# Layer 0's preparation: two blocks' destination terms formed on VectorE, their values deferred

## The chip, the cores and the metric

The kernel runs on one core of one Trainium2 chip. The metric is device time in microseconds for one launch, the median over runs. A profiled execution of the same program gives the trace that this document reads. In its lines PE is TensorE (PEld its weight loads), DVE is VectorE, ACT is ScalarE, POOL is GpSimd and SP is SyncE.

## What is computed

The reference is a stack of four graph layers over 4096 nodes with 256 features and one sparse 0/1 adjacency matrix. Each layer normalises its input and applies ReLU first. Only layer 0 is touched:

```python
h = jnp.maximum(_layernorm(x, axis=-1), 0.0)
Wh = h @ W
e = Wh @ a_src + (Wh @ a_dst).T          # logit of (row i, column j)
e = jnp.where(e > 0, e, 0.2 * e)         # leaky ReLU
e = jnp.where(adj > 0, e, -9.0e15)
attn = jax.nn.softmax(e, axis=1)
h_attn = attn @ Wh
```

After this comes the dense rest of layer 0, then layers 1 (mean over neighbours), 2 (attention again) and 3 (dot-product attention).

## The kernel before

Nodes are handled in 32 tiles of 128, and four tiles make a block, so there are 8 blocks (`NB = 8`, `BT = 4`, `NT = 32`). Layer 0's attention has two stages.

**The preparation**, the subject of this case, is the function `block0(b)`, run for the 8 blocks as staggered generators. For a block it takes the statistics of its four rows of x on VectorE (`stats_of`, L130 and L131). It subtracts the mean with its sign turned, xs = mean − x: two of the four tiles on GpSimd (the first and the last), one on ScalarE (L803), one on VectorE (all the others at L807). It computes 1/std on GpSimd (`rstd_of`, L121 and L124, into `pl_rs`). TensorE transposes the block (L153, into `tp`), and ScalarE evacuates the transposes with ReLU and scale −1 (L155, into `hT`). TensorE then multiplies each tile with `w2` (L162, into `mm`), which holds W and two more columns W·a_src and W·a_dst, and ScalarE scales the product by 1/std into `v` (`project`, L310). So `v` holds, for each node, its value row and its terms src and dst. The two extra columns of `w2` are formed by VectorE in `columns` (L296), for which TensorE spreads the two vectors (L289).

Between these steps the adjacency is unpacked. `load` asks for units of 128 rows by 1024 columns through GpSimd's DMA queue (L639). `fresh` transposes a unit on TensorE (L649, into `cT`), and ScalarE turns it with an Exp into a code that separates edges from non-edges (L654, into `turned`). A group of 4 row tiles has 16 units.

VectorE then runs, for each group, over all 32 column tiles and keeps the running minimum of (code − dst): `reach` (L335 and L337, into `run`, and the last one into `run_sb`). This gives each row's maximum of dst over its neighbours. Column tile j needs its dst and the code of its quarter. Transposed and reduced (`top`: L358, L362 to L367), it becomes two numbers for each row, which are spread over the partitions by TensorE (L372, L387) and copied (L376, L392).

**The loop** `run` then forms for each pair of column tiles the logits on VectorE (L412), subtracts the code on GpSimd (L418, L420), takes Exp on ScalarE (L482) and accumulates the weighted values on TensorE (L505, into `acc`). While it does so for one group, `ahead` unpacks the units of the next group and VectorE reaches over it.

Each engine takes its instructions in one fixed order. That order is made when the program is built: a scheduler places the instructions that the Python code records, and `tc.issue_after(x)` asks that what is recorded inside it stands behind x on its queue. `psm` has two buffers for the products `mm`, so TensorE can be at most two tiles ahead of their evacuation. `work` has two buffers, `small` four.

Of the kernel before, what the change touches and what calls it, by code (L numbers as in the profile page):

```python
# [11 lines left out]
F32 = mybir.dt.float32  # L12
# [31 lines left out]
def kernel(ctx: ExitStack, tc: tile.TileContext, w: dict, out: bass.AP):  # L44
# [101 lines left out]

    def transposed_block(work, pst, h, tag, turned=None):

        hT = work.tile([P, KD, BW], F32, tag=tag, name=tag)
        for k in range(KD):  # L150
            ps = pst.tile([P, BW], F32, tag="tp", name="tp")
            for i in range(BT):
                nc.tensor.transpose(ps[:, ts(i, P)], h[:, i, ts(k, P)], ident)  # L153
            if turned is not None:
                turned.append(nc.scalar.activation(hT[:, k, :], ps, AF.Relu, scale=-1.0))  # L155
            else:
                evac(k, hT[:, k, :], ps)
        return hT

    def products(ps, lhsT_of, rhs_of, n):  # L160
        for k in range(n):
            nc.tensor.matmul(  # L162
                out=ps, lhsT=lhsT_of(k), rhs=rhs_of(k), start=(k == 0), stop=(k == n - 1)
            )

    PE, DVE = "PE", "DVE"
# [48 lines left out]
    class Attention:  # L215
        def __init__(self, es, tag, slope, lag, n_y, blocks, turned, finish, ps_top=None):
            self.tag, self.slope, self.lag, self.n_y = tag, slope, lag, n_y
            self.turned, self.finish = turned, finish

            self.links = []  # L220
            self.blocks = [{"at": at, "n": n} for at, n in blocks]
            vp = es.enter_context(tc.tile_pool(reuse_waits="tile", name=f"{tag}_sd", bufs=1))
            self.sdst = vp.tile([P, NT], F32, name="sdst")
            self.cdst = vp.tile([P, NT], F32, name="cdst")
            self.own_dst, self.held = None, False
# [65 lines left out]
        def columns(self, work):  # L291
            w2, a2 = self.w2, self.a2
            for k in range(KD):
                for v in range(2):
                    junk = work.tile([P, D], F32, tag="junk", name="junk")
                    nc.vector.tensor_tensor_reduce(  # L296
                        junk, w2[:, k, 0:D], a2[:, ts(v, D)], 1.0, 0.0, ALU.mult, ALU.add,
                        w2[:, k, D + v : D + v + 1],
                    )

        def project(self, b, hT, psm, rs=None):

            for i in range(BT):
                ps = psm.tile([P, D + 2], F32, tag="mm", name="mm")
                products(ps, lambda k: hT[:, k, ts(i, P)], lambda k: self.w2[:, k, :], KD)
                row = self.v[:, b * BT + i, 1 : D + 3]
                if rs is None:
                    nc.scalar.copy(row, ps)
                else:
                    nc.scalar.mul(row, ps, rs[:, i : i + 1])  # L310

        def slopes(self, at):
            dst = self.dst_of(at)
            nc.vector.tensor_scalar(self.sdst[:, at], dst, self.slope, None, ALU.mult)
            nc.vector.tensor_scalar(self.cdst[:, at], dst, 1.0 - self.slope, None, ALU.mult)

        def reach(self, n, tie=None):
# [9 lines left out]
            for j in range(c, c + 2):  # L327
                code = self.turned(b, j // QT)[:, :, j % QT, :]
                dst = self.dst_of(slice(j, j + 1)) if tie is None else tie[:, j - c : j - c + 1]
                to = st["run"]  # L330
# [19 lines left out]
        def top(self, b, pool=None, tag="top"):  # L350
# [6 lines left out]
            for r in range(n):  # L357
                nc.tensor.transpose(ps[:, r, :], st["run"][:, r, :], ident)  # L358
            yield DVE
# [18 lines left out]
            if b < self.spread:  # L378

                yield PE  # L380
                for v in range(2):
# [4 lines left out]
                    for k in range(n):  # L386
                        nc.tensor.matmul(  # L387
                            out=ps[:, k, :], lhsT=self.picks[0 : 2 * n, v * n + k, :], rhs=abT,
# [16 lines left out]
        def logits(self, y, b, c, mask):  # L405
# [5 lines left out]
            for k in range(2):  # L411
                nc.vector.scalar_tensor_tensor(  # L412
                    y[k], st["ab"][:, 0, :, :], self.cdst[:, c + k : c + k + 1],
                    st["b"], ALU.add, ALU.max,
                )
                if y.apart:
                    eng = (nc.vector, nc.gpsimd)[k]
                    ins = eng.tensor_tensor(y[k], y[k], mask[:, :, c % QT + k, :], ALU.subtract)  # L418
            if not y.apart:
                ins = nc.gpsimd.tensor_tensor(  # L420
                    y.both, y.both, mask[:, :, c % QT : c % QT + 2, :], ALU.subtract
                )
            return ins

# [5 lines left out]
        def run(self, es, goal, n_acc, ahead=lambda n: None):  # L430
# [15 lines left out]
            for n in range(len(pairs) + LAG):  # L446
                between = False
                if n < len(pairs):
# [21 lines left out]
                    ys[n] = y  # L470
                    masked = self.logits(y, b, c, self.turned(b, c // QT))
                    if n < PPB and not self.tied:
                        with tc.issue_after((self.newest if n > LAG else masked).ins):
                            ahead(n)
                        while self.reached <= m:
                            self.reach(self.reached)
                if n >= LAG:
                    b, c = pairs[n - LAG]
                    y = ys.pop(n - LAG)
                    with tc.issue_after(self.gate.ins) if self.gate and c else ExitStack():  # L480
                        for k in range(2):
                            self.newest = nc.scalar.activation(  # L482
                                y[k], y[k], AF.Exp,
                                bias=self.sdst[:, c + k : c + k + 1],
                            )
                    if c == 0:
                        accs[b] = [
# [88 lines left out]
    FIRST = UPB  # L576
    FRESH = 3
    UNITS0 = (0, 2, 4, 6, 8, 11, 14, 16)
    PAIRS0 = (0, 0, 0, 2, 4, 6, 8, 12, 16)
    PACE = (LAG0 + 1, 2 * PPB + 4)  # L580
    with ExitStack() as l0:
# [10 lines left out]
        with ExitStack() as es:  # L592
# [14 lines left out]
            def turned_of(k, q):  # L607
# [12 lines left out]
            att.picks, att.spread = picks.tile([n, n, P], F32, name="picks"), 2  # L620
            nc.vector.tensor_copy(
                att.picks,
                ident[0:n, 0:n].rearrange("k (v o) -> k v o", o=1).broadcast_to([n, n, P]),
            )
            adj_p = es.enter_context(tc.tile_pool(reuse_waits="tile", name="adj", bufs=8))
# [5 lines left out]
            ]  # L631
            raw, made = [], [0]

# [7 lines left out]
            def fresh(up_to):  # L641

                load(up_to)
                for g in range(made[0], up_to):
# [3 lines left out]
                    for i in range(QW // BW):  # L648
                        nc.tensor.transpose(ps[:, ts(i, P)], words[:, ts(i, P)], ident)  # L649
                    if (b, q) not in turned:  # L650
# [117 lines left out]
            with ExitStack() as ps_:  # L768
# [11 lines left out]
                for at, n in [(0, BT // 2), (BT // 2, BT // 2)] + [  # L780
# [5 lines left out]
                    )  # L786

                def block0(b):
                    xb = xs[:, ts(b, BT), :]
                    mv = small.tile([P, BT, 2], F32, tag="pl_mv", name="pl_mv")  # L790
                    for i in range(BT):
                        st = None
                        if b == 0:

                            st = work.tile([P, D], F32, tag="junk", name="junk")[:, 0:6]
                        stats_of(small, xb[:, i, :], mv[:, i, :], "pl", st)


                    for i in range(BT):
                        mean = mv[:, i, 0:1]  # L800
                        if i == 1 or b == 0 and i == BT - 1:
                            with tc.issue_after(evacs[-1].ins) if evacs else ExitStack():
# [3 lines left out]
                        else:  # L806
                            (nc.gpsimd if b and i in (0, BT - 1) else nc.vector).tensor_scalar(  # L807
                                xb[:, i, :], xb[:, i, :], mean, -1.0, ALU.subtract, ALU.mult
                            )
                    rs = rstd_of(small, mv, BT, "pl")  # L810
                    if b == 0:
                        att.spread_row(a_row, psm)
                        att.columns(work)
                    load(min(3 * b + 6, UPB + RB))
                    yield
                    hT = transposed_block(work, pst, xb, "hT", turned=evacs)
                    fresh(UNITS0[b])
                    yield
                    att.project(b, hT, psm, rs)
                    yield  # L820
# [5 lines left out]
                run_staggered([block0(b) for b in range(NB)], 2)  # L826
                for _ in att.top(0, pst, "tp"):
                    pass
                att.held = False
                att.slopes(slice(0, NT))  # L830
                fresh(UPB + 2)
# [726 lines left out]
```

## Time and profile before

| what | value |
|---|---|
| runs, us | 2859.99, 2856.09, 2857.85 |
| median, us | 2857.85 |
| the profiled execution's own time, us | 2859.48 |
| its span, us | 2857.7 |
| granted TensorE clock, mean over the span | 0.994 |
| busy: PE / DVE / ACT / POOL | 98% / 67% / 44% / 35% |
| chain that ended last: PE | 84% |

The span is what the trace covers; 1.78 us of the profiled time lie around it. The profiled execution is 1.63 us above the median. TensorE is busy nearly all the time but for the first slices, so the shares over the whole span say little of the preparation, which ends some 70 us after the start: there one has to read windows and the order of time.

### The profile page before, as it was taken

To read this page: it belongs to the slowest core of one execution; us is meant where nothing else is said; L and a number is where in the kernel's file an instruction comes from. 1 tells how busy PE (TensorE), PEld (TensorE's weight loads), DVE (VectorE), ACT (ScalarE), POOL (GpSimd) and SP (SyncE) were. 2 spreads that over 40 slices of the span, in tenths; PEclk is the share of its full clock that TensorE was granted. 3 is DMA by queue.
4 is the path that set the end of the run, shared out by engine and by line. 5 is a ranking of instruction groups with operands and counts; after the bars stand their busy time and mean duration, and the time that the engine had idled before them with its cause. 6 is when DMAs were issued, how large, how long until landed. Compare 5 with 4: busy or idle time off the path is not lost.

```text
span 2857.7 us, 33849 instructions
## 1 busy us (share of the span) xinstructions
PE 2802.7 (98%) x12614; PEld 2298.7 (80%) x12614; DVE 1910.2 (67%) x3441; ACT 1249.4 (44%) x1883; POOL 1005.0 (35%) x901
## 2 busy tenths in 40 slices
PE   7999999999999999999999999999999999999999
PEld 5888888856666666888788888878888888888888
DVE  6877777345555555677799999547666665666563
ACT  6666654366777753787444444441211121112111
POOL 5767766445555553221076666610000000000000
PEclk9999999999999999999999999999999999999999
DMA  7988884322233312799322221021110101111100
GB/s 170 148 176 167 164 165 138 86 19 26 26 28 30 29 15 79 149 203 202 143 82 91 94 82 52 8 71 47 47 38 33 63 33 38 34 53 43 37 4 8
DMA packets 102327, 223.05 MB, mean 78 GB/s; under 512 B 10562, under 2 KB 52276, under 8 KB 91156
## 3 DMA queue, kind: packets, MB, share of 16 engines
q1 hardware_dynamic: 63072, 181.39, 17.9%
q0 software_dynamic: 37536, 35.03, 15.5%
q10 hardware_dynamic: 1556, 4.49, 0.4%
q8 instruction: 99, 1.62, 0.2%
q14 instruction: 64, 0.52, 0.1%
HBM read 264.85 MB, written 56.68 MB: 113 GB/s over the span
## 4 chain that ended last, share of the span: by engine, by line
PE 84%; DVE 5%; POOL 3%; ACT 3%; issue 3%; DMA 1%; POOLq 0%; ACTq 0%; DVEq 0%; SPq 0%
PE acc L505 22%; PE mm L162 19%; PE acc L1490 16%; PE s L162 15%; PE acc L1225 8%; POOL y L420 2%; DVE run L337 2%; PE tp L877 2%; DVE y L412 1%; ACT y L482 1%; ACT turned L654 1%; PE q_ps L162 1%; DMA ab_row<-l_ab_d 1%; POOL adj_t L639 1%; DMA l_ab_d<-abT_sb 0%
## 5 line engine op out<-in xcount | busy, mean ns | idle before, releaser
L505 PE MATMUL acc<-v,y 128*128 128x257 f32 x4096 | 913.8, 382 | 8.4 <-ACT y L482 7.6
L505 PEld LDWEIGHTS acc<-v,y 128*128 128x128 f32 x4096 | 772.6, 191 | 116.0 <-ACT y L482 8.6
L420 POOL TENSOR_TENSOR y<-y,turned 128x1024 f32<-128x1024 f32 x255 | 543.0, 2136 | 288.7 <-DVE y L412 194.9
L482 ACT ACTIVATE y<-y,sdst 128x512 f32<-128x512 f32 x512 | 342.5, 714 | 377.7 <-POOL y L420 375.4
L1490 PE MATMUL acc<-v,y 128*128 128x257 f32 x2048 | 454.5, 380 | 0.4 <-DVE rden L1498 0.4
L162 PE MATMUL s<-qT,hT 128*128 128x256 f32 x2048 | 445.2, 379 | 0.7 <-ACT qT L1438 0.7
L1483 ACT ACTIVATE y<-y 128x1024 f32<-128x1024 f32 x128 | 132.5, 1055 | 714.8 <-DVE y L1482 710.5
L162 PEld LDWEIGHTS s<-qT,hT 128*128 128x128 f32 x2048 | 389.0, 190 | 54.1 <-ACT qT L1438 1.3
L1490 PEld LDWEIGHTS acc<-v,y 128*128 128x128 f32 x2048 | 387.1, 190 | 55.9 <-issue 0.8
L412 DVE SCALAR_TENSOR_TENSOR y<-ab_row,cdst,b 128x512 f32<-128x512 f32 x512 | 362.6, 742 | 70.1 <-PE acc L505 61.4
L192 ACT ACTIVATE sign<-a,limits 128x1024 bf16<-128x1024 fp8e5 x256 | 293.7, 1147 | 7.1 <-DMA a<-in_adj_dram 1.1
L1452 DVE SCALAR_TENSOR_TENSOR y<-code,s 128x512 f32<-128x512 bf16 x256 | 175.8, 687 | 101.1 <-PE s L162 101.0
L337 DVE SCALAR_TENSOR_TENSOR run<-turned,v,run 128x512 f32<-128x512 bf16 x240 | 180.2, 751 | 48.1 <-ACT turned L654 45.7
L1482 DVE TENSOR_TENSOR y<-y,top 128x1024 f32<-128x1024 f32 x128 | 146.2, 1214 | 30.4 <-PE top L1476 30.4
L183 POOL DMA_DIRECT2D a<-in_adj_dram x128 | 76.0, 597 | 248.1 <-ACT sign L192 210.4
L1459 DVE TENSOR_TENSOR mx<-mx,y 128x512 f32<-128x512 f32 x224 | 154.8, 691 | 7.5
L654 ACT ACTIVATE turned<-cT,log_wide 128x1024 bf16<-128x1024 fp8e5 x128 | 139.2, 1105 | 27.2 <-PE cT L649 26.9
L337 DVE SCALAR_TENSOR_TENSOR run<-turned,y,run 128x512 f32<-128x512 bf16 x193 | 145.2, 753 | 3.0
L162 PE MATMUL mm<-kept 128*128 128x512 f32 x288 | 130.4, 595 | 0.0
L1225 PE MATMUL acc<-early,eq 128*128 128x512 f32 x512 | 126.4, 397 | 0.3 <-DVE o L1234 0.3
L1498 DVE RECIPROCAL rden<-acc 128x1 f32<-128x1 f32 x32 | 5.2, 163 | 177.8 <-PE acc L1490 177.8
L1225 PE MATMUL acc<-late,eq 128*128 128x512 f32 x512 | 122.4, 391 | 0.0
(256 smaller groups left out, 3130.8 us busy)
## 6 DMA issues: line engine op xcount, KB each, us to landing
codesT<-turned SPq DMA_DIRECT2D x50, 1024.0 KB, 5.9
turned<-codesT SPq DMA_DIRECT2D x36, 1024.0 KB, 4.8
code<-codesT SPq DMA_DIRECT2D x128, 256.0 KB, 6.5
code<-codesT SPq DMA_DIRECT2D x64, 512.0 KB, 6.4
adj_t<-in_adj_dram POOLq DMA_DIRECT2D x128, 128.0 KB, 6.0
a<-in_adj_dram POOLq DMA_DIRECT2D x128, 128.0 KB, 4.6
xt<-in_x_dram SPq DMA_DIRECT2D x8, 512.0 KB, 3.2
ab_row<-l_ab_d ACTq DMA_DIRECT2D x8, 512.0 KB, 3.6
```

The lines of the kernel that those rows point to most:

```text
L162: nc.tensor.matmul(out=ps, lhsT=lhsT_of(k), rhs=rhs_of(k), start=(k == 0), stop=(k == n - 1))
L192: nc.scalar.activation(sign, self.came[g], AF.Sign, bias=limits[:, v : v + 1], accum_out=over[:, t, v, q : q + 1],)
L337: nc.vector.scalar_tensor_tensor(to, code, dst, st["run"], ALU.subtract, ALU.min)
L412: nc.vector.scalar_tensor_tensor(y[k], st["ab"][:, 0, :, :], self.cdst[:, c + k : c + k + 1], st["b"], ALU.add, ALU.max,)
L420: ins = nc.gpsimd.tensor_tensor(y.both, y.both, mask[:, :, c % QT : c % QT + 2, :], ALU.subtract)
L482: self.newest = nc.scalar.activation(y[k], y[k], AF.Exp, bias=self.sdst[:, c + k : c + k + 1],)
L505: nc.tensor.matmul(out=accs[b][r], lhsT=y1[j % 2][:, r, :], rhs=self.v[:, j, 0 : D + 1], start=(j == 0), stop=(j == NT - 1),)
L654: nc.scalar.activation(ct.rearrange("p (g k) i -> p g k i", k=4), ps.bitcast(F8).rearrange("p (g i k) -> p g k i", i=P, k=4), AF.Exp, scal ...
L1225: nc.tensor.matmul(out=acc, lhsT=eqs[c // (NT // 2)][:, ts(c % (NT // 2), P)], rhs=v1[c // BT][:, c % BT, :, :], start=(c == 0), stop=(c = ...
L1452: nc.vector.scalar_tensor_tensor(y[:, :, c : c + 2, :], st["code"][:, :, c : c + 2, :], -BIG / UNIT, ps, ALU.mult, ALU.add,)
L1459: nc.vector.tensor_tensor(mx, mx, y[:, :, c : c + 2, :], ALU.max)
L1490: nc.tensor.matmul(out=accs[r], lhsT=st["y"][:, r, c, :], rhs=v3[:, c, :], start=(c == 0), stop=(c == NT - 1),)
```

## The change

In layer 0's preparation:

- For the last two blocks (b = 6 and 7, `near`) the mean is subtracted with its own sign and ReLU is applied in the same instruction, no tile of them goes to ScalarE, and `transposed_block` is given scale +1.
- For these blocks dst is not read from the product with `w2`. VectorE multiplies each of the eight tiles with a row `wa` (W·a_dst laid along the free axis on all partitions) and sums (`tensor_tensor_reduce`, changed L853), then scales by 1/std (changed L856), into `near`. `reach` reads `near` for the last eight column tiles.
- `wa` comes from two more TensorE products in block 1 (changed L864) and a ScalarE copy (changed L868).
- The products and values of the two blocks are recorded after all the blocks, behind the newest unit transposed, and the last tile behind the transposes of `top`.
- In blocks 4 and 5 two of the four value tiles are scaled out of PSUM by VectorE instead of ScalarE (changed L314).
- `columns` comes ahead of the statistics of blocks 1 to 7 in VectorE's queue, and the copy to `picks` behind it. `load` asks for up to 24 units in the preparation instead of 20.
- In the loop, `ahead` of the first four pairs comes behind the Exp of the first pair, `reach` stands behind the newest logits, and the two subtractions of the first pair are recorded in the other order.

The diff, cut to what matters:

```diff
-    def transposed_block(work, pst, h, tag, turned=None):
+    def transposed_block(work, pst, h, tag, turned=None, sign=-1.0):
...
-                turned.append(nc.scalar.activation(hT[:, k, :], ps, AF.Relu, scale=-1.0))
+                turned.append(nc.scalar.activation(hT[:, k, :], ps, AF.Relu, scale=sign))
...
-        def project(self, b, hT, psm, rs=None):
-
-            for i in range(BT):
+        def project(self, b, hT, psm, rs=None, rows=range(BT), shared=False):
+
+            for i in rows:
...
+                elif shared and i % 2:
+                    nc.vector.tensor_scalar(row, ps, rs[:, i : i + 1], None, ALU.mult)
                 else:
                     nc.scalar.mul(row, ps, rs[:, i : i + 1])
...
-                dst = self.dst_of(slice(j, j + 1)) if tie is None else tie[:, j - c : j - c + 1]
+                if b == 0 and self.near is not None and j >= NT - NEAR * BT:
+                    at_near = j - NT + NEAR * BT
+                    dst = self.near[:, at_near : at_near + 1]
+                else:
+                    dst = self.dst_of(slice(j, j + 1)) if tie is None else tie[:, j - c : j - c + 1]
...
                     if n < PPB and not self.tied:
-                        with tc.issue_after((self.newest if n > LAG else masked).ins):
-                            ahead(n)
-                        while self.reached <= m:
-                            self.reach(self.reached)
+                        if n > LAG:
+                            with tc.issue_after(self.newest.ins):
+                                ahead(n)
+                        with tc.issue_after(self.on_dve.ins):
+                            while self.reached <= m:
+                                self.reach(self.reached)
...
+                    if n == LAG and not self.tied:
+                        with tc.issue_after(self.newest.ins):
+                            for k in range(n + 1):
+                                ahead(k)
...
+    NEAR = 2
...
+                att.near = wp.tile([P, NEAR * BT], F32, name="near")
+                wa = wp.tile([P, D], F32, name="wa0")
+                formed, kept_back = [], []
+
                 def block0(b):
                     xb = xs[:, ts(b, BT), :]
+                    near = b >= NB - NEAR
                     mv = small.tile([P, BT, 2], F32, tag="pl_mv", name="pl_mv")
-                    for i in range(BT):
+                    with tc.issue_after(formed[0].ins) if formed else ExitStack():
+                        for i in range(BT):
...
                     for i in range(BT):
                         mean = mv[:, i, 0:1]
-                        if i == 1 or b == 0 and i == BT - 1:
+                        eng = nc.gpsimd if b and i in (0, BT - 1) else nc.vector
+                        if near:
+                            eng.tensor_scalar(
+                                xb[:, i, :], xb[:, i, :], mean, 0.0, ALU.subtract, ALU.max
+                            )
+                        elif i == 1 or b == 0 and i == BT - 1:
...
                     if b == 0:
                         att.spread_row(a_row, psm)
-                        att.columns(work)
-                    load(min(3 * b + 6, UPB + RB))
+                        formed.append(att.columns(work))
+                        with tc.issue_after(formed[0].ins):
+                            nc.vector.tensor_copy(att.picks, one_of)
+                    load(min(3 * b + 6, UPB + 2 * RB))
...
-                    att.project(b, hT, psm, rs)
+                    if near:
+                        to = att.near[:, (b - NB + NEAR) * BT :][:, 0:BT]
+                        for i in range(BT):
+                            junk = work.tile([P, D], F32, tag="junk", name="junk")
+                            nc.vector.tensor_tensor_reduce(
+                                junk, xb[:, i, :], wa, 1.0, 0.0, ALU.mult, ALU.add, to[:, i : i + 1]
+                            )
+                        nc.vector.tensor_tensor(to, to, rs, ALU.mult)
+                        kept_back.append((b, hT, psm, rs))
+                    else:
+                        att.project(b, hT, psm, rs, shared=b >= NB - NEAR - 2)
+                    if b == 1:
+                        ps = psm.tile([P, D], F32, tag="mm", name="mm")
+                        for k in range(KD):
+                            col = att.w2[:, k, D + 1 : D + 2]
+                            nc.tensor.matmul(
+                                out=ps[:, ts(k, P)], lhsT=col.broadcast_to([P, P]), rhs=ident,
+                                start=True, stop=True,
+                            )
+                        nc.scalar.copy(wa, ps)
...
                 run_staggered([block0(b) for b in range(NB)], 2)
-                for _ in att.top(0, pst, "tp"):
+                att.slopes(slice(0, NT - NEAR * BT))
+                att.slopes(slice(NT - NEAR * BT, NT), att.near)
+                with tc.issue_after(newest_unit[0].ins):
+                    att.project(*kept_back[0])
+                    att.project(*kept_back[1], rows=range(0, BT - 1))
+                chain = att.top(0, pst, "tp")
+                for _ in range(2):
+                    next(chain)
+                with tc.issue_after(att.on_pe.ins):
+                    att.project(*kept_back[1], rows=range(BT - 1, BT))
+                for _ in chain:
                     pass
                 att.held = False
-                att.slopes(slice(0, NT))
                 fresh(UPB + 2)
```

More of the change, by code (lines that the diff above doesn't have):

```diff
@@ L161, in products @@
         for k in range(n):
-            nc.tensor.matmul(
+            last = nc.tensor.matmul(
                 out=ps, lhsT=lhsT_of(k), rhs=rhs_of(k), start=(k == 0), stop=(k == n - 1)
             )
+        return last
     PE, DVE = "PE", "DVE"
@@ L224, in __init__ @@
             self.cdst = vp.tile([P, NT], F32, name="cdst")
-            self.own_dst, self.held = None, False
+            self.own_dst, self.held, self.near = None, False, None
             self.tied = False
@@ L295, in columns @@
                     junk = work.tile([P, D], F32, tag="junk", name="junk")
-                    nc.vector.tensor_tensor_reduce(
+                    last = nc.vector.tensor_tensor_reduce(
                         junk, w2[:, k, 0:D], a2[:, ts(v, D)], 1.0, 0.0, ALU.mult, ALU.add,
@@ L299, in columns @@
                     )
-        def project(self, b, hT, psm, rs=None):
-            for i in range(BT):
+            return last
+        def project(self, b, hT, psm, rs=None, rows=range(BT), shared=False):
+            for i in rows:
                 ps = psm.tile([P, D + 2], F32, tag="mm", name="mm")
-                products(ps, lambda k: hT[:, k, ts(i, P)], lambda k: self.w2[:, k, :], KD)
+                self.projected = products(
+                    ps, lambda k: hT[:, k, ts(i, P)], lambda k: self.w2[:, k, :], KD
+                )
                 row = self.v[:, b * BT + i, 1 : D + 3]
@@ L308, in project, with slopes @@
                     nc.scalar.copy(row, ps)
+                elif shared and i % 2:
+                    nc.vector.tensor_scalar(row, ps, rs[:, i : i + 1], None, ALU.mult)
                 else:
                     nc.scalar.mul(row, ps, rs[:, i : i + 1])
-        def slopes(self, at):
-            dst = self.dst_of(at)
+        def slopes(self, at, dst=None):
+            dst = self.dst_of(at) if dst is None else dst
             nc.vector.tensor_scalar(self.sdst[:, at], dst, self.slope, None, ALU.mult)
@@ L357, in top @@
             for r in range(n):
-                nc.tensor.transpose(ps[:, r, :], st["run"][:, r, :], ident)
+                self.on_pe = nc.tensor.transpose(ps[:, r, :], st["run"][:, r, :], ident)
             yield DVE
@@ L386, in top @@
                     for k in range(n):
-                        nc.tensor.matmul(
+                        self.on_pe = nc.tensor.matmul(
                             out=ps[:, k, :], lhsT=self.picks[0 : 2 * n, v * n + k, :], rhs=abT,
@@ L411, in logits @@
             for k in range(2):
-                nc.vector.scalar_tensor_tensor(
+                self.on_dve = nc.vector.scalar_tensor_tensor(
                     y[k], st["ab"][:, 0, :, :], self.cdst[:, c + k : c + k + 1],
@@ L415, in logits @@
                 )
[L416 to L420, printed above, removed]
+            if y.apart:
+                nc.gpsimd.tensor_tensor(y[1], y[1], mask[:, :, c % QT + 1, :], ALU.subtract)
+                self.on_dve = nc.vector.tensor_tensor(
+                    y[0], y[0], mask[:, :, c % QT, :], ALU.subtract
+                )
+            else:
+                nc.gpsimd.tensor_tensor(
                     y.both, y.both, mask[:, :, c % QT : c % QT + 2, :], ALU.subtract
                 )
-            return ins
         def open_b(self, es):
@@ L470, in run @@
                     ys[n] = y
-                    masked = self.logits(y, b, c, self.turned(b, c // QT))
+                    self.logits(y, b, c, self.turned(b, c // QT))
                     if n < PPB and not self.tied:
-                        with tc.issue_after((self.newest if n > LAG else masked).ins):
-                            ahead(n)
-                        while self.reached <= m:
-                            self.reach(self.reached)
+                        if n > LAG:
[4 more added lines that the diff above has]
+                                self.reach(self.reached)
                 if n >= LAG:
@@ L620 @@
             att.picks, att.spread = picks.tile([n, n, P], F32, name="picks"), 2
[L621 to L624, printed above, removed]
+            one_of = ident[0:n, 0:n].rearrange("k (v o) -> k v o", o=1).broadcast_to([n, n, P])
             adj_p = es.enter_context(tc.tile_pool(reuse_waits="tile", name="adj", bufs=8))
@@ L631 @@
             ]
-            raw, made = [], [0]
+            raw, made, newest_unit = [], [0], [None]
             def load(up_to):
@@ L648, in fresh @@
                     for i in range(QW // BW):
-                        nc.tensor.transpose(ps[:, ts(i, P)], words[:, ts(i, P)], ident)
+                        newest_unit[0] = nc.tensor.transpose(ps[:, ts(i, P)], words[:, ts(i, P)], ident)
                     if (b, q) not in turned:
@@ L786 @@
                     )
+                att.near = wp.tile([P, NEAR * BT], F32, name="near")
+                wa = wp.tile([P, D], F32, name="wa0")
+                formed, kept_back = [], []
                 def block0(b):
                     xb = xs[:, ts(b, BT), :]
+                    near = b >= NB - NEAR
                     mv = small.tile([P, BT, 2], F32, tag="pl_mv", name="pl_mv")
-                    for i in range(BT):
[L792 to L796, printed above, removed]
+                    with tc.issue_after(formed[0].ins) if formed else ExitStack():
+                        for i in range(BT):
+                            st = None
+                            if b == 0:
+                                st = work.tile([P, D], F32, tag="junk", name="junk")[:, 0:6]
+                            stats_of(small, xb[:, i, :], mv[:, i, :], "pl", st)
                     for i in range(BT):
                         mean = mv[:, i, 0:1]
-                        if i == 1 or b == 0 and i == BT - 1:
+                        eng = nc.gpsimd if b and i in (0, BT - 1) else nc.vector
[4 more added lines that the diff above has]
+                        elif i == 1 or b == 0 and i == BT - 1:
                             with tc.issue_after(evacs[-1].ins) if evacs else ExitStack():
@@ L806, in block0 @@
                         else:
-                            (nc.gpsimd if b and i in (0, BT - 1) else nc.vector).tensor_scalar(
+                            eng.tensor_scalar(
                                 xb[:, i, :], xb[:, i, :], mean, -1.0, ALU.subtract, ALU.mult
@@ L812, in block0 @@
                         att.spread_row(a_row, psm)
-                        att.columns(work)
-                    load(min(3 * b + 6, UPB + RB))
+                        formed.append(att.columns(work))
+                        with tc.issue_after(formed[0].ins):
+                            nc.vector.tensor_copy(att.picks, one_of)
+                    load(min(3 * b + 6, UPB + 2 * RB))
                     yield
-                    hT = transposed_block(work, pst, xb, "hT", turned=evacs)
+                    hT = transposed_block(
+                        work, pst, xb, "hT", turned=evacs, sign=1.0 if near else -1.0
+                    )
                     fresh(UNITS0[b])
                     yield
-                    att.project(b, hT, psm, rs)
+                    if near:
[4 more added lines that the diff above has]
+                                junk, xb[:, i, :], wa, 1.0, 0.0, ALU.mult, ALU.add, to[:, i : i + 1]
+                            )
+                        nc.vector.tensor_tensor(to, to, rs, ALU.mult)
+                        kept_back.append((b, hT, psm, rs))
+                    else:
+                        att.project(b, hT, psm, rs, shared=b >= NB - NEAR - 2)
[6 more added lines that the diff above has]
+                                start=True, stop=True,
+                            )
+                        nc.scalar.copy(wa, ps)
                     yield
```

## The prediction

> **What bounds the kernel now.** I read the busy shares first. TensorE's 98% says that no other engine can bound the whole, so what the preparation gives or takes shows in the total only as far as it shifts the start of TensorE's unbroken work. Then windows (columns: stretch; us, then busy us and instructions of PE/PEld/DVE/ACT/POOL; granted clock, DMA share, GB/s):
>
> ```profile
> PE 2802.7 (98%) x12614; PEld 2298.7 (80%) x12614; DVE 1910.2 (67%) x3441; ACT 1249.4 (44%) x1883; POOL 1005.0 (35%) x901
> ```
> ```profile
> 20.00:30.00 10.00, 9.80 (x56) 8.05 (x55) 7.14 (x25) 10.00 (x19) 9.63 (x14) 1.00 1.12 135
> 30.00:40.00 10.00, 10.00 (x54) 7.97 (x53) 5.26 (x8) 9.14 (x17) 9.61 (x14) 1.00 1.09 181
> 50.00:60.00 10.00, 7.43 (x38) 5.72 (x37) 7.17 (x13) 7.83 (x14) 0.00 (x0) 1.00 0.26 107
> 60.00:70.00 10.00, 5.27 (x21) 4.28 (x21) 4.04 (x10) 2.86 (x4) 0.49 (x1) 0.51 0.05 19
> 83.00:117.00 34.00, 34.00 (x170) 29.70 (x169) 29.50 (x45) 27.68 (x37) 28.99 (x24) 1.00 1.00 157
> 64.00:68.00 4.00, 3.78 (x16) 3.48 (x16) 0.04 (x1) 1.84 (x4) 0.00 (x0) 0.50 0.00 0
> ```
>
> ScalarE is full from 20 to 30 and close to it after, GpSimd is at 96% until 40, VectorE at 53 to 71%. So ScalarE paces the blocks, and GpSimd is nearly as full. From 83 on TensorE has no gap: a shift there is carried to the end. Last, the order of time (start, us, engine and line):
>
> ```profile
> 37.41 2.27 POOL L807 TENSOR_SCALAR xs<-xs,pl_mv 128x256 f32<-128x256 f32 x2
> 37.42 6.30 DVE L337 SCALAR_TENSOR_TENSOR run<-turned,v,run 128x512 f32<-128x512 bf16 x8 [4.53 <-ACT turned L654]
> 40.14 2.28 POOL L807 TENSOR_SCALAR xs<-xs,pl_mv 128x256 f32<-128x256 f32 x2
> 57.72 0.48 ACT L310 ACTIVATE v<-mm,pl_rs 128x258 f32<-128x258 f32 x1 [0.36 <-PE mm L162]
> 60.00 0.75 DVE L337 SCALAR_TENSOR_TENSOR run_sb<-turned,v,run 128x512 f32<-128x512 bf16 x1
> 67.97 1.40 DVE L412 SCALAR_TENSOR_TENSOR y<-ab_row,cdst,b 128x512 f32<-128x512 f32 x2 [4.65 <-PE b L387]
> 70.93 1.72 POOL L639 DMA_DIRECT2D adj_t<-in_adj_dram  x3
> 72.40 2.94 PE L505 MATMUL acc<-v,y 128*128 128x257 f32 x6 [4.54 <-ACT y L482]
> 82.32 3.73 PE L505 MATMUL acc<-v,y 128*128 128x257 f32 x16 [0.60 <-ACT y L482]
> ```
>
> GpSimd reaches block 6 at 37.41 and block 7 at 40.14. The last v ends at 58.20, run_sb at 60.75, and 7.22 later the first logits start. The first sixteen of the loop's products (6 + 6 + 4 in the trace) take from 72.40 to 82.32, 9.9 where the next sixteen take 3.7: transposes of adjacency asked for only at 70.93 come between them, and the clock stands at 0.5.
>
> **What the change saves.** ScalarE loses two subtractions, about 2 x 0.42, and four values of blocks 4 and 5, 4 x 0.38; it defers eight values, 8 x 0.38, and gains one copy, 0.4: 5.0 us less ahead of the last run (0.38 and 0.42 are my estimates, below the 0.48 of the single v above for the overlap of neighbours). With ScalarE still the bound, run_sb would come about 4.5 earlier, the last runs being VectorE's own.
>
> **What the change makes VectorE wait for.** In the built queue, block 6's four products with `wa` (L853) stand ahead of the very first run. The first of them needs GpSimd's subtraction of that block's first tile. GpSimd's queue ahead of it is the old one plus one more load (21 instead of 20). In before that subtraction starts at 37.41 in an engine without gaps, so it starts at 37.4 + 0.6 = 38.0 (a load holds GpSimd 1.72 / 3) and ends at 38.0 + 2.27 / 2 = 39.1. VectorE has nothing else: block 6's statistics and its own subtractions are done near 23. It stands about 15 us, where in before it had run eight runs by 43.7. Behind it are queued all 32 runs, block 7's statistics and the four values taken from ScalarE. TensorE's products use two buffers, so when a value of block 4 sits behind VectorE, TensorE stands within two tiles, and ScalarE, which waits for its transposes, with it.
>
> From 39.1, VectorE's own work up to run_sb:
> - 32 runs at 6.30 / 8 = 0.787: 25.2.
> - 8 products, 0.35 each: 2.8. No row has this operation with wa; an early one of the same kind took 0.40 and VectorE's 128x256 scaling out of PSUM 0.48, so the bounds are 0.33 to 0.48, at most 1.0 more. I take the low end, since these stand back to back.
> - Block 7's statistics 1.5, two subtractions 0.7, four values 4 x 0.45 = 1.8, slopes 0.6, two scalings 0.2.
>
> Sum 32.8: run_sb cannot end before 71.9. In order: four products with four runs between, 43.1, scaling 43.6; block 7's statistics among the next four runs, 47.9. Only then has GpSimd block 7's means (in before at 40.14): its subtractions and 1/std end near 50.4, so VectorE's last product of block 7 and the scaling reach 50.6. The other 24 runs 18.9, the four values less the overlap 1.6, slopes 0.5: 71.6. Meanwhile TensorE and ScalarE have stood from about 39 to 51 with 7 of 16 units unturned; starved values of block 4 and 5 cost VectorE some 2.6 and one late unit 0.9. End of run_sb near **75.0 instead of 60.75, +14.2**; without these waits +11.
>
> **From there to steady work.** The chain to the first logits is 7.2 in before, with its spreads at half clock:
>
> ```profile
> 64.08 2.07 PE L387 MATMUL spread<-abT_sb,picks 8*128 8x128 f32 x8 [0.34 <-ACT abT_sb L376]
> 65.95 1.91 PE L387 MATMUL b<-abT_sb,picks 8*128 8x128 f32 x8
> ```
>
> At full clock these 4 us halve, 7.2 − 1.9 = 5.3 in all. [...] Only the last deferred tile lies inside `top` (behind its transposes); the other seven are placed behind the newest unit, so they come earlier. First logits: 75.0 + 5.3 to 7.2 = 80.3 to 82.2, +12.3 to +14.2. The products then gain: units 20 to 23 are asked for in the preparation too, so the requests after 70.93 and their flights no longer stand in the way. Of the excess 9.9 − 3.7 = 6.2, I take 4.0 (the wait at 75 to 80 and the slow clock are not wholly the loads). Net +8.3 to +10.2, middle **+9**; bounds: +11 with all saved and full clock is 11 − 2 − 6.2 = +3, and +14.2 + 1.0 with nothing regained is +15.
>
> A walk through the five built queues with the trace's durations, an estimate, gives before's run_sb start at 59.6 (trace 60.0) and first logits at 67.3 (67.97); the changed queues give 73.8 to 74.4, 79.1 to 81.5, and the third sixteen products 8 to 11 later; with durations and clock varied, 3 to 16.
>
> [...] **Clock:** the window 64 to 68 has TensorE busy 3.78 of 4.00 and still 0.50. [...] **Shared access:** GpSimd's pair at 37.41 took 2.27 with VectorE's runs beside it, and 2.28 at 40.14. [...]
>
> **What costs nothing, and under which cover.** `columns` leading brings the first product from 12.65 to about 9.1, but the next bound is GpSimd's queue, which was gapless; the 1.4 and the picks copy (0.8) delay block 1's statistics by 2.2, and its subtraction on GpSimd, at 10.17 in before, by 0.5. Two more products and the copy of `wa`, 0.5 each at most, lie under the wait until 39. The three further extra loads, 3 x 0.6 on GpSimd, stand behind block 6's subtraction, while GpSimd waits for block 7's means anyway; uncovered they cost 1.7. The same four are missing later. SP's store of the first turned units goes out later and no one waits for it before the next layer. From about 170 us on the order on every engine is as before.
>
> **Rivals.**
> (a) *The stall is there, most of it absorbed.* Full clock through recovery, no starved values, and nearly all of the 6.2 saved: +2 to +5, 2860 to 2863. For it: the 9.9 of the first sixteen products. Against: TensorE has 12 us to stand still in.
> (b) *Faster.* ScalarE stays the bound. This needs block 6's first subtraction on GpSimd to end by about 28 instead of 39.1, since VectorE's own 32.8 then end within 61, and by 24 for the whole gain. Price: 4.5 earlier, and 4 in the first sixteen products: −8.5, 2849. Against it: GpSimd 9.63 and 9.61 of 10 busy, and nothing taken out of its queue. It could come only if GpSimd's instructions ran much shorter beside an idle VectorE.
> (c) *Half clock throughout recovery:* values of 0.5 us wait longer for products at half speed and the deferred ones stretch `top`: +14 to +16, 2873.
> (d) *It does not do what it says:* the deferred products lie not in the chain but mostly ahead of it; if they came after run_sb instead, 7 x 0.7 at half clock would add 4.9, at the upper end of (c).
>
> **Numbers.** The sum is made on the profiled execution, 2859.48; it is 1.63 above the median, so +9 gives 2868.5 there and 2866.9 on the median: 2867. Chances: forecast 0.70 (2863.5 to 2872), (a) 0.15, (b) 0.11, (c) and (d) 0.04. The forecast's own range is 2863 to 2872; with (a) and most of (c) 2856 to 2874, which leaves out (b) and a little more. A measurement tells about 0.2%, 5.7 us: below 2852.1 is faster, 0.11; to 2863.6 same, 0.17 (a and the forecast's low edge); above 0.72.
>
> **What would show it.** Right: VectorE idle some 15 us ahead of L853, released by GpSimd's xs at 38 to 39; TensorE and ScalarE thin from 39 to 51; run_sb ending at 73 to 76; first logits at 79 to 83; no wait for adjacency among the first sixteen products, and the second sixteen from 89 to 93; TensorE full after it. Wrong: the first L853 before 30, or run_sb before 66.

## The result and the profile after

The changed kernel takes 2866.77 us (median of 11 runs, 2864.81 to 2870.43); the kernel before, run beside it, 2858.4. The ratio is 1.0025, 95% interval [1.0017, 1.0033], so 8 us slower at a forecast of 9. The profiled execution took 2868.61, its span is 2866.8 (before: 2859.48 and 2857.7).

The profile's busy times moved by under 7 us on any engine, and TensorE's not at all (2802.7 us in both), so the loss is idle time of TensorE. The windows (columns as in the prediction) show where:

```profile
PE 2802.7 (98%) x12618; PEld 2298.5 (80%) x12618; DVE 1916.8 (67%) x3467; ACT 1248.0 (44%) x1878; POOL 1005.7 (35%) x901
```
```profile
20.00:30.00 10.00, 9.85 (x56) 7.98 (x54) 3.69 (x18) 9.14 (x18) 9.55 (x14) 1.00 1.10 202
30.00:40.00 10.00, 6.44 (x33) 4.90 (x32) 0.58 (x3) 7.38 (x13) 9.65 (x14) 0.93 1.10 165
40.00:50.00 10.00, 0.00 (x0) 0.00 (x0) 9.67 (x32) 0.00 (x0) 6.60 (x9) 0.50 1.04 133
52.00:56.00 4.00, 3.20 (x11) 2.72 (x12) 3.27 (x7) 0.22 (x1) 0.00 (x0) 0.50 0.00 0
56.00:60.00 4.00, 4.00 (x17) 3.34 (x16) 1.96 (x4) 2.86 (x4) 0.00 (x0) 0.63 0.00 0
60.00:64.00 4.00, 3.65 (x26) 3.09 (x25) 2.41 (x7) 2.83 (x5) 0.00 (x0) 1.00 0.00 0
94.00:128.00 34.00, 33.89 (x167) 29.41 (x166) 30.59 (x47) 26.48 (x35) 32.34 (x24) 1.00 0.86 139
```

From 30 to 40 VectorE does 0.58 us of work (before 5.26); from 40 to 50 it is full, and TensorE and ScalarE do nothing at all. The clock is 0.50 in 40 to 50 and in 52 to 56, 0.63 in 56 to 60 and 1.00 in 60 to 64. From 94 on TensorE is full, as it was from 83 before. The order of time (start, us, engine, line; in brackets the idle time ahead and its releaser) names each wait; the lines are a choice from several engines:

```profile
38.23 1.16 POOL L824 TENSOR_SCALAR xs<-xs,pl_mv 128x256 f32<-128x256 f32 x1
39.42 0.43 DVE L853 CUSTOM_DVE_ANT_0 junk<-xs,wa 128x256 f32<-128x256 f32 x1 [15.44 <-POOL xs L824]
...
43.79 0.16 DVE L856 TENSOR_TENSOR near<-near,pl_rs 128x4 f32<-128x4 f32 x1 [0.26 <-POOL pl_rs L124]
...
48.28 1.67 POOL L824 TENSOR_SCALAR xs<-xs,pl_mv 128x256 f32<-128x256 f32 x1 [2.00 <-DVE pl_mv L131]
51.33 0.16 DVE L856 TENSOR_TENSOR near<-near,pl_rs 128x4 f32<-128x4 f32 x1 [0.92 <-POOL pl_rs L124]
52.80 2.09 PE L162 MATMUL mm<-w,hT 128*128 128x258 f32 x4 [15.24 <-DVE v L314]
...
59.63 0.49 DVE L314 TENSOR_SCALAR v<-mm,pl_rs 128x258 f32<-128x258 f32 x1 [1.97 <-PE mm L162]
...
75.82 0.75 DVE L347 SCALAR_TENSOR_TENSOR run_sb<-turned,near,run 128x512 f32<-128x512 bf16 x1
79.34 1.15 PE L397 MATMUL spread<-abT_sb,picks 8*128 8x128 f32 x8 [0.34 <-ACT abT_sb L386]
80.34 1.05 PE L397 MATMUL b<-abT_sb,picks 8*128 8x128 f32 x8
81.50 1.41 DVE L422 SCALAR_TENSOR_TENSOR y<-ab_row,cdst,b 128x512 f32<-128x512 f32 x2 [2.82 <-PE b L397]
86.06 2.94 PE L522 MATMUL acc<-v,y 128*128 128x257 f32 x6 [2.17 <-ACT y L495]
89.21 2.59 PE L522 MATMUL acc<-v,y 128*128 128x257 f32 x10
91.86 3.63 PE L522 MATMUL acc<-v,y 128*128 128x257 f32 x16
```

VectorE stands 15.44 us for GpSimd's subtraction of block 6. TensorE then stands 15.24 for a value that VectorE, busy with what it had put off, scales only at 52.27. `run_sb` ends at 76.57 (60.75), the first logits start at 81.50 (67.97), and the second sixteen products at 91.86 (82.32).

### The profile page after: what moved, and what is told of

It reads as the page before. It is cut to its first block, busy times and chain, and to the rows that moved or that the text cites. A ratio compares the mean times of both kernels' runs of the same rounds, so it can differ in the third digit from the quotient of the medians.

```text
span 2866.8 us, 33871 instructions
## 1 busy us (share of the span) xinstructions
PE 2802.7 (98%) x12618; PEld 2298.5 (80%) x12618; DVE 1916.8 (67%) x3467; ACT 1248.0 (44%) x1878; POOL 1005.7 (35%) x901
## 4 chain that ended last, share of the span: by engine, by line
PE 88%; POOL 4%; DVE 3%; issue 2%; ACT 2%; DMA 1%; POOLq 0%; ACTq 0%; SPq 0%; DVEq 0%
PE acc L522 26%; PE mm L162 18%; PE acc L1548 15%; PE s L162 15%; PE acc L1283 8%; PE tp L935 2%; POOL y L432 2%; DVE run L347 1%; PE q_ps L162 1%; ACT y L495 1%; PE cT L664 1%; DMA xs<-in_x_dram 0%; POOL pl_rs L124 0%; ACT turned L669 0%; DVE y L422 0%
```

## The experiments

All times are medians with the kernel before run beside them. The theory is the prediction's: VectorE, taking its queue in order, stands for things that GpSimd makes late. The rivals: the price is VectorE's added work, or the change's other parts cost.

| run | us | before beside it | ratio, 95% interval | run_sb ends | second sixteen products |
|---|---|---|---|---|---|
| e1_behind | 2867.07 | 2860.06 | 1.0022 [1.0013, 1.0030] | 74.09 | 90.92 |
| e2_behind_buf8 | 2852.19 | 2860.06 | 0.9972 [0.9961, 0.9982] | 59.68 | 75.59 |
| e3_no_near | 2851.93 | 2860.06 | 0.9970 [0.9959, 0.9982] | 58.61 | 75.97 |
| e4_no_share | 2862.46 | 2860.06 | 1.0009 [1.0000, 1.0018] | 70.90 | 89.80 |
| e5_edges | 2863.15 | 2860.46 | 1.0008 [0.9999, 1.0017] | 70.14 | 87.25 |
| e6_no_near_no_lead | 2870.68 (one run) | 2860.46 | none | 73.83 | 88.92 |
| e7_no_near_old_loads | 2856.04 | 2860.46 | 0.9987 [0.9978, 0.9995] | 58.90 | 79.97 |
| e8_share_no_near | 2851.80 | 2860.46 | 0.9967 [0.9957, 0.9977] | 57.93 | 74.72 |
| e9_lead_undone | 2854.77 | 2860.65 | 0.9978 [0.9969, 0.9988] | 60.05 | 78.00 |
| e10_near_no_waits | 2848.42 | 2860.65 | 0.9958 [0.9944, 0.9971] | 58.62 | 75.24 |
| e11_old_loads | 2873.44 | 2860.65 | 1.0043 [1.0027, 1.0059] | 73.89 | 92.23 |
| e12_no_waits_no_share | 2852.69 | 2859.14 | 0.9976 [0.9966, 0.9986] | 58.74 | 74.06 |

The last two columns are read from each run's trace; the changed kernel has 76.57 and 91.86, the kernel before 60.75 and 82.32.

**e1_behind: the near products moved behind.**

```diff
-    for i in range(BT): ... tensor_tensor_reduce(junk, xb[:, i, :], wa, ...)
-    nc.vector.tensor_tensor(to, to, rs, ALU.mult)
+    with tc.issue_after(att.last_run.ins):      # the newest L347 recorded
+        (the same instructions)
```

> The near products (L853, L856 of the change) are asked to stand behind the last run recorded so far, all else as changed. Theory in its simplest form (only their place ahead of the first run costs): VectorE's 15 us are gone, run_sb ends at 59 to 60, time 2850 to 2853 where the kernel before has 2858. Walk of the built queues: the first run starts at 25.6, but VectorE then stands some 14 us at the means of block 7, whose buffer (one of four) GpSimd gives back only near 40; run_sb at 72 to 75, 2864 to 2867. Rival 'it is VectorE's added work': no idle of that size on VectorE, 2865 to 2867.

Moved alone, the products gain nothing. The first run starts at 23.89, but the place of the old wait is taken by a new one (VectorE, order of time):

```profile
42.12 0.18 DVE L131 BATCH_NORM_AGGREGATE pl_mv<-pl_st 128x2 f32<-128x6 f32 x1 [17.48 <-POOL pl_ve L121]
```

Block 7's means wait for the buffer that GpSimd's L121 reads. The simplest form of the theory fell here: the place ahead of the first run was one of two waits behind one another, and the second alone is enough for nearly the whole loss (1.0022, the change 1.0025).

**e2_behind_buf8: and the buffer too.** `l0_ps` with `bufs=8` instead of 4.

> As the run before it, and eight buffers instead of four for the means and the other small tiles, so that block 7's statistics need not wait. Theory (VectorE's order and what GpSimd gives late, not the work): run_sb starts at 59 to 61, first logits at 66 to 67, time 2851 to 2854, faster than before (2858). Rival 'VectorE's added work': the work is all still there, 2863 to 2867.

VectorE, order of time:

```profile
58.93 0.75 DVE L348 SCALAR_TENSOR_TENSOR run_sb<-turned,near,run 128x512 f32<-128x512 bf16 x1
```

`run_sb` ends 17 us earlier than in the changed kernel, and the same instructions are all there (3467 on VectorE in both). The rival of VectorE's work is out: the loss was waiting.

**e3_no_near: only the other parts.** `near = False`, `shared=False`, nothing kept back, one `att.slopes(slice(0, NT))`.

> The two parts named in the change's first half are left out: no dst by VectorE, no deferred values, and the values of blocks 4 and 5 on ScalarE; what stays is W's columns leading, 24 units asked for and the order in the loop. Theory: these cost nothing and save some, by the walk run_sb starts at 58.0 against 59.6 before and the products start 5 to 7 earlier: 2851 to 2853. Rival 'the other parts cost': 2858 to 2867. My prediction's own pricing (columns at nothing, 4 regained in the first sixteen products): 2854.

The other parts cost nothing; they save 0.30%. The near half of the change, as built, took that back and 0.25% more. The chain's state is seen in TensorE's order of time:

```profile
61.48 2.07 PE L397 MATMUL spread<-abT_sb,picks 8*128 8x128 f32 x8 [0.34 <-ACT abT_sb L386]
63.35 1.91 PE L397 MATMUL b<-abT_sb,picks 8*128 8x128 f32 x8
...
69.80 2.94 PE L522 MATMUL acc<-v,y 128*128 128x257 f32 x6 [2.86 <-ACT y L495]
```

Without the deferred values the spreads took 2.07 and 1.91 again, as in the kernel before, where the clock was 0.50 in 64 to 68; in the changed kernel they took 1.15 and 1.05, at 1.00 in 76 to 82. That the deferred values alone decide this is not shown: e5_edges below has them and the same 2.07 and 1.91.

**e4_no_share: the four values back on ScalarE.** `shared=False`.

> The changed kernel with the four values of blocks 4 and 5 on ScalarE again. Theory: VectorE still stands some 15 us ahead of the first near product, but TensorE and ScalarE do not stand with it and the values' own 1.8 and starved 3.3 are gone: run_sb starts at 67 to 71 instead of 75.8, time 2861 to 2864. Rival 'VectorE's wait for GpSimd is all': 2866 to 2867 as changed.

The near product still starts late, at 39.63, but ScalarE works on until 47 and `run_sb` ends 5.7 earlier: 1.8 of work and 3.3 of starved values (0.73 + 1.97 + 0.57 in the changed kernel) make 5.1. So the stall had two parts, VectorE's own and the one it passes on.

**e5_edges: block 6's subtraction off GpSimd.** `eng = nc.gpsimd if b and not near and i in (0, BT - 1) else nc.vector`.

> The changed kernel with the first and last tile of blocks 6 and 7 subtracted on VectorE instead of GpSimd, so that the first near product has nothing of GpSimd to wait for; its scaling by 1/std (L856), which GpSimd still forms, stays where it was. Theory: the first near product starts near 26 instead of 39.4, but VectorE then stands at the scaling of block 6 until GpSimd's 1/std comes, some 5 us earlier than before; run_sb starts at 68 to 71, time 2861 to 2864. Rival 'only the products' wait counts': VectorE stands nowhere long, 2851 to 2854.

The first near product starts at 24.67, and VectorE then stands at the next thing of GpSimd's (VectorE, order of time), 2.7 us earlier than in the changed kernel, not the 5 expected:

```profile
41.09 0.16 DVE L856 TENSOR_TENSOR near<-near,pl_rs 128x4 f32<-128x4 f32 x1 [12.31 <-POOL pl_rs L124]
```

That is the third wait of the same row: subtraction, buffer of the means, 1/std. The chain is not short in this run, though its deferred values are where the change put them (TensorE, order of time):

```profile
73.02 2.07 PE L397 MATMUL spread<-abT_sb,picks 8*128 8x128 f32 x8 [0.34 <-ACT abT_sb L386]
74.89 1.91 PE L397 MATMUL b<-abT_sb,picks 8*128 8x128 f32 x8
```

**e6_no_near_no_lead: the changed kernel without the lead of W's columns.** The `issue_after(formed[0].ins)` around the statistics is left out. The label says too much: the near products are in.

> The changed kernel with W's columns no longer made to lead VectorE's queue (the statistics of blocks 1 to 7 are free to stand ahead of them). My prediction priced the lead at nothing; theory says the same here, since GpSimd's subtraction of block 6 comes first: the first run within 1 us of the change's 39.8 and the time within 2 us of it.

The first run starts at 39.82 (39.77), so up to there the lead was worth nothing, as priced. Behind it the trace is not the same: block 7's scaling came at 49.12 instead of 51.33 and `run_sb` 2.7 earlier. The one time is 2.1 above the profiled one of the change: inconclusive on the total.

**e9_lead_undone: the same in e3_no_near.**

> As e3_no_near, and W's columns no longer made to lead VectorE's queue. The prediction priced the lead at nothing because block 6's near products wait for GpSimd; where these are gone ScalarE paces, and the first product 3.5 to 4 us earlier should count: by the walk the first run starts at 26.6 against 24.9, run_sb at 59.7 against 58.0, products 2 to 2.6 later, 2854 to 2855. Rival 'the lead is worth nothing anywhere': as e3_no_near, 2852.

The first product starts at 12.09 (9.15 in e3_no_near), the second sixteen at 78.00 (75.97). With the near stall gone the lead is worth 2.0 us in the trace; the intervals of the two totals overlap (0.9978 and 0.9970), and their difference, 2.3, agrees.

**e7_no_near_old_loads: 20 units asked for and the old order in the loop.** `load(min(3 * b + 6, UPB + RB))`; `run` and `logits` as before.

> As e3_no_near, and 20 units asked for in the preparation and the old order in the loop; of the change only W's columns leading is left. By the walk run_sb starts at 58.0 as in e3_no_near, but the first sixteen products again take 9.5 to 10 instead of some 6, so 3 to 4 us above e3_no_near: 2854 to 2856. Rival 'the loads are hidden': as e3_no_near.

TensorE, order of time:

```profile
70.04 2.94 PE L515 MATMUL acc<-v,y 128*128 128x257 f32 x6 [4.54 <-ACT y L492]
73.22 0.69 PE L657 MATMUL cT<-ident,adj_t 128*128 128x128 f32 x2 [0.24 <-DMA adj_t<-in_adj_dram]
74.47 0.69 PE L657 MATMUL cT<-ident,adj_t 128*128 128x128 f32 x2 [0.57 <-DMA adj_t<-in_adj_dram]
...
79.97 3.73 PE L515 MATMUL acc<-v,y 128*128 128x257 f32 x16 [0.63 <-ACT y L492]
```

The first sixteen products take 9.9 again, 6.2 in e3_no_near, the two waits for adjacency with them: 3.8 us from loads and order together.

**e11_old_loads: the same in the changed kernel.**

> The changed kernel with 20 units asked for in the preparation and the old order in the loop. The prediction's +0.6 for one more load ahead of GpSimd's subtraction and its -4.0 for the first sixteen products are tried at once: the near product starts 0.6 to 1.6 earlier (37.8 to 38.8), the first sixteen products take 9 to 10 instead of 5.8; time 2867 to 2871. Rival 'the loads of the loop are hidden behind the late start': as the change or 1 us less, 2866 to 2867.

Both prices were tried. The near product starts at 37.31, 2.1 earlier (0.6 to 1.6 expected). Only 0.6 of it is the load: block 5's 1/std, 1.06 on GpSimd, also stands behind block 6's subtraction here, ahead of it in the change. The first sixteen take 9.0 instead of 5.8. The total is above the expected range, and the excess lies further on. Products 129 to 512 of the loop (windows of that stretch; kernel before, the change, this run):

```profile
108.67:203.73 95.06, 93.74 (x471) 80.75 (x469) 76.13 (x125) 60.41 (x80) 63.83 (x52) 1.00 0.83 167
```
```profile
118.49:212.01 93.52, 93.27 (x470) 80.85 (x469) 74.99 (x125) 61.48 (x81) 64.99 (x52) 1.00 0.84 170
```
```profile
118.58:214.96 96.38, 93.96 (x471) 80.66 (x469) 76.13 (x125) 60.36 (x80) 63.85 (x52) 1.00 0.83 165
```

The same products take 95.06, 93.52 and 96.38; TensorE's idle time in them is 1.3, 0.3 and 2.4. With the new loads and order and no near products (e3_no_near) it is 93.55, with the old ones (e7_no_near_old_loads) 95.44. So they save 1.5 to 2.9 us there as well; which of the two was not separated.

**e8_share_no_near: the values on VectorE without the near products.** e3_no_near with `shared=b in (4, 5)`.

> As e3_no_near, but four values of blocks 4 and 5 are VectorE's again. Theory: without the near products ahead of them VectorE reaches these values in time, ScalarE, which paces the blocks, is 1.5 us shorter, run_sb starts at 56.9 against 58.0, time 0 to 1.5 us under e3_no_near: 2850 to 2852. Rival 'a value behind VectorE's runs starves TensorE whatever stands ahead': 2 to 5 above e3_no_near.

`run_sb` 0.7 earlier than in e3_no_near; the times cannot be told apart. Where no stall stands ahead of them, the values on VectorE starve nobody (from 20 to 58 TensorE waits for none of them): the 5.7 us of e4_no_share were the price of the stall, handed on to TensorE.

**e10_near_no_waits: all of the change, its three waits taken away.** The edit of e5_edges, `bufs=8`, and L856 alone inside `issue_after(att.last_run.ins)`.

> All of the change is kept, with its near products where they were, and only their waits are taken away: edge tiles of blocks 6 and 7 on VectorE (as e5_edges), the scaling L856 behind the last run recorded, eight small buffers. Theory: e5_edges plus the two remaining waits gone; VectorE has no idle of more than 4 us, run_sb starts at 58 to 60, time 2851 to 2854. Rival 'a third cost in the near products': 2856 or more.

2848.42, 0.42% faster than before, and lower than expected. VectorE works 18.94 of the 20 us from 20 to 40 (4.26 in the changed kernel, 20.00:40.00 of both):

```profile
20.00:40.00 20.00, 18.59 (x103) 15.12 (x102) 18.94 (x62) 17.48 (x32) 19.27 (x27) 1.00 1.10 186
```
```profile
20.00:40.00 20.00, 16.29 (x88) 12.87 (x86) 4.26 (x21) 16.53 (x30) 19.20 (x27) 0.96 1.10 184
```

**e12_no_waits_no_share: the same with `shared=False`.**

> As e10_near_no_waits, with the four values of blocks 4 and 5 on ScalarE again. Theory: without VectorE's waits it is of no account where the four values stand (walk: run_sb starts at 58.0 here, 58.2 there), so within 2 us of e10_near_no_waits: 2847 to 2852 by the same kernel before. Rival 'ScalarE's 1.5 us count': 2 to 3 slower. If it lies above 2853, e10_near_no_waits was a lucky draw.

Its products start 1.2 earlier in the trace, its time is 4 us higher; the intervals just overlap. By its ratio it would stand at 2853.8 beside the kernel before of e10_near_no_waits (2860.65): above the 2853 that the expectation named as the sign of a lucky draw. So e10_near_no_waits beats the kernel before and the changed one, but that it beats e12_no_waits_no_share, or e3_no_near and e8_share_no_near, which have no near products, is not shown. No run shows a gain from the near products themselves.

## Why the prediction was right, point by point

- **GpSimd's time.** The subtraction of block 6 was put at 38.0 to 39.1: 38.23 to 39.39. VectorE's "about 15" of standing: 15.44. One row beside it was misread, without weight in the sum: by 43.7 the kernel before had done sixteen runs, not eight (the first at 26.47).
- **VectorE's order after it.** Scaling of block 6 at 43.6: 43.79. Block 7's statistics done at 47.9: 48.19. Its near row done at 50.6: 51.49, 0.9 late, 0.3 of it with the statistics and 0.5 because GpSimd's last subtraction took 1.67 and not 1.15.
- **Starved values and the late unit.** 2.6 and 0.9 forecast; 3.27 and 0.88. With the 0.9 above this makes the whole miss at `run_sb`: 76.57 instead of 75.0 (+15.8, not +14.2), which is also outside the 73 to 76 named as a sign of being right.
- **The chain.** 5.3 to 7.2 forecast, 4.93 measured, 0.4 under my lower end, with the clock at 1.00 throughout (76 to 82). First logits at 81.50, inside 80.3 to 82.2. That it was the short end was luck. With the deferred values the chain took 4.9 in this kernel and (labels shortened) e6, e10, e11 and e12, and 5.7 in e2, but 6.8 to 7.5 in e1, e4 and e5; without them (e3, e7, e8, e9) it took 6.7 to 7.2. The spreads took 1.15 and 1.05 in e11, 2.07 and 1.91 in e5 and e3. What decides between them is open. With the longer chain the change would have cost some 2 us more (an estimate from these numbers), still inside the range.
- **The first sixteen products.** 4.0 of 6.2 regained forecast, 4.1 measured (9.92 to 5.80). e7_no_near_old_loads and e11_old_loads show that the loads and the loop's order make it, not the late start.
- **The sum.** +15.8 at `run_sb`, −2.3 in the chain, +0.1 to the first product, −4.1 in the products: +9.5 at the second sixteen, where +8.3 to +10.2 stood. So the miss at `run_sb` (+1.6) was made good chiefly by the chain, 1.3 below the middle of its range: the total was nearer than its terms. The rest I took as a mere shift. It was not quite one: +0.3 to product 129, −1.5 over products 129 to 512 and +0.8 behind them leave +9.1 for the whole span.
- **Rival (b), faster.** Its condition was too weak. I asked only for an early subtraction of block 6; e5_edges gave that, 15 us earlier, and was not faster than the kernel before. Block 7's buffer and 1/std have to come as well. With all three the gain is 12 us in e10_near_no_waits (0.42% of 2858) and 7 in e12_no_waits_no_share. That is near the 8.5 that this rival was priced at, but not by its terms: `run_sb` came 2.1 and 2.0 earlier, not 4.5, and as much in e3_no_near, where ScalarE is not relieved at all. That the work taken from ScalarE is worth 4.5 us is not borne out; most of the gain is behind `run_sb`.
- **Columns at nothing.** True under the stall as far as the first run (e6_no_near_no_lead), open behind it, where that run's `run_sb` came 2.7 earlier; without the stall the lead is worth 2 us in the trace (e9_lead_undone). A price of zero was the cover's, not the step's.
- **The clock and GpSimd's subtractions.** In the changed kernel the last product ahead of the stall ended at 37.56 and the next began at 52.80; the clock was 0.76 in 38 to 39, 0.50 in 39 to 59 and 1.00 in 59 to 82, so it came back some 6 us after TensorE had begun again. In the kernel before it was 1.00 in 20 to 60, 0.58 in 60 to 61, 0.50 in 61 to 80 and 0.68 in 80 to 81. What sets these moments is not shown. The sum left the chain's clock open, 5.3 or 7.2, and the short end came. On GpSimd's subtractions see the last section.

## What to carry to other kernels

Before an instruction is given to an engine with free time, look at where the built queue puts it, and price everything behind it with the lateness of its slowest input; busy shares do not show this. When a wait is taken away, ask for the next one of the same producer: here subtraction, buffer and 1/std of one full engine stood behind one another, and with one of them gone most of the loss was left (1.0022 in e1_behind and 1.0008 in e5_edges; the change 1.0025, e3_no_near without near products 0.9970). A step that looks free under a stall is to be priced again without it.

## What was not expected of the hardware

GpSimd was no quicker beside an idle VectorE: 1.16 for the subtraction at 38.23, against 2.27 for two at 37.41 in the kernel before, with VectorE's runs beside them. But some near products and subtractions of GpSimd's that overlap took longer than the others. In e2_behind_buf8, first VectorE's near products, then GpSimd in the same stretch:

```profile
42.96 0.42 DVE L855 CUSTOM_DVE_ANT_0 junk<-xs,wa 128x256 f32<-128x256 f32 x1
43.30 0.83 DVE L855 CUSTOM_DVE_ANT_0 junk<-xs,wa 128x256 f32<-128x256 f32 x1
...
44.47 0.79 DVE L855 CUSTOM_DVE_ANT_0 junk<-xs,wa 128x256 f32<-128x256 f32 x1
45.20 0.41 DVE L855 CUSTOM_DVE_ANT_0 junk<-xs,wa 128x256 f32<-128x256 f32 x1
```
```profile
43.38 2.26 POOL L825 TENSOR_SCALAR xs<-xs,pl_mv 128x256 f32<-128x256 f32 x2
```

Two products that lie beside the subtractions (43.38 to 45.64) take 0.83 and 0.79, the one ahead of them 0.42; GpSimd's pair took its usual 2.26. The last one, at 45.20 in the pair's final 0.44 us, took 0.41; why is not shown. In the changed kernel one product, at 48.94, took 0.61 and the subtraction beside it, at 48.28, 1.67; but VectorE's own two subtractions, at 48.10, lie beside that one too, and at 40.53, with products and runs but no subtraction beside it, one took 1.32. The three slow products (0.83, 0.79, 0.61) have a subtraction of GpSimd's beside them, but so have four in the changed kernel, at 40.43, 41.43, 48.60 and 49.48, which took 0.41 or 0.42; that the overlap is the cause is not shown. If it is, it cost by these rows, an estimate, some 0.2 us on VectorE in the changed kernel (0.61 − 0.42), and on GpSimd 0.2 at 40.53 (1.32 − 1.15) and at most 0.5 at 48.28 (1.67 − 1.15); no run measured it by itself. The prediction's sum took one length for a product (0.35) and one for a subtraction (2.27 / 2), whatever stands beside it.
